# The second mixture's early results: kept in DRAM and scattered after the gathers

## The chip, the core and the metric

The kernel runs on one core of a Trainium2 chip. The metric is the device time of one execution in microseconds: 2697.74 us is the median of three runs of the kernel before (2694.27, 2697.74 and 2700.65). A core has five engines that run side by side: TensorE (PE in the profile, with PEld for its weight loads), VectorE (DVE), ScalarE (ACT), GpSimd (POOL) and SyncE (SP). SP does no arithmetic here; it issues plain DMAs. POOL issues the indirect DMAs, those with an index for each of 128 rows, and does little else. [...]

## The reference, cut to what matters

Two graph layers and two mixtures of experts alternate on 6250 nodes of 256 features (100,000 edges). The change lies in the last two of the four:

```python
x = x + _L1_gnn_ref(_layernorm(x), edge_index, W, att_src, att_dst, bias)   # attention over each node's edges
x = x + _L1_ffn_ref(_layernorm(x)[None], Wg, bg, W1, b1, W2, b2)[0]         # mixture, 8 experts, the best 2

def _L1_ffn_ref(x, Wg, bg, W1, b1, W2, b2):
    gate_logits = xf @ Wg + bg
    top_w, top_i = jax.lax.top_k(gate_logits, 2)
    top_w = softmax(top_w)
    ...
    for e in range(8):
        h = gelu(xf @ W1[e] + b1[e])                 # 256 -> 1024
        out = out + w_dense[:, e:e+1] * (h @ W2[e] + b2[e])   # 1024 -> 256
```

## The kernel before, in words

**Stages.** The first layers, their routing and the preparation of the edges come first. `gnn1` then writes a table `t1_d` to DRAM: for each node its projected features, its attention scores and its x. Nodes are sorted by degree into 49 tiles of 128, and tile t needs `CAPS[t]` gathers (8 to 41, 813 in all), one for each edge place. The stage of the change, `ffn1` (from L1202), does the attention and the second mixture in one pipelined loop. At its end the output stage (L1383 on, tiles `yg`) adds the two results that each node has in `parts` and writes `out`.

**One step of the loop** (s = 0, 1, ...; `while` at L1290) does a bit of several things, and the order is written out by hand for all engines (`manual_schedule`): each engine gets its instructions in the order in which the code makes them.
- `gather` (L1004): POOL gathers the node's own row (`own`, L1010) and then K = `CAPS[t]` tiles of 128 rows into `g` (L1020) for the tile of this step. After each gather `between()` takes one item from `outbox`. What is left in `outbox` after the last gather is issued with a small memset `gap` ahead of each (L1369).
- The attention of the tile gathered one step before (`q1`): `scores` and `shares` on DVE and ACT, `messages` on DVE (L1065), and `total` on PE (L1071, L1074), two matmuls for each gather, into `sums`.
- The end of the attention for the tile before that (`q2`): `result` on DVE, layer norm (its square root on ACT, L368), the normed `xn` (L1317), two transposes on PE (`pT`, L1320), and the gate's logits (L1225).
- Every few steps a group of four tiles is complete. `choose`, `count`, `place` and `listed` find its two experts for each node and their places (`slot`, L617), and eight row scatters `f_rows<-rw,slot` (L625), two for each tile, are put into `outbox` for the next step. They write the normed rows into a table with a region for each expert. A later group makes more blocks of 256 rows due (`moe.due`), and `written` turns their list (`blk`) on PE (L684).
- One block of 256 rows of one expert for each step, in three steps one after another. As `new`: SP fetches its rows `xr` (L697), `bcol` (L699), `ob` (L701) and the first weights w1 (1 MB, L1231), and ACT and PE turn the rows (`bxn` L1267, `bxT` L711). As `cur`: SP fetches the second weights w2 (1 MB, L1238), and `inner` (L1248, 32 matmuls `ph`) and the gelu on ACT (L1252) make `hT`. As `prev`: `outer` (L1259, 32 matmuls `py`), and `put` (L734 on ACT, L735 and L737 on DVE) makes the two results `by`. A DMA of SP also waits for the one issued eight before it.
- `sends`: the two scatters `f_parts<-by,btok` of the block (L742) are put into `outbox` for the next step. `btok` (L726) holds for each row the place in `parts`; each place is written once.

PE's order in a step is thus: `py`, two `pT`, `ph`, four `pT`, the gate, `sums`. There are 49 steps with gathers (0 to 48) and 56 blocks. A group is gathered every four steps, so its eight row scatters are in the queue of every fourth step: 16, 20, 24, ... 48. Block 0 is put at step 15 and the next ones from step 19 on, one a step. After step 48 no gathers are left; the last small groups are chosen, `nulls` (L641) fills the rest of the experts' regions, and the remaining blocks follow one a step, to step 73.

**Buffers.** `g` has 5 (two for each step from K = 14 on), `own` 4, `by` 4, w1 and w2 two each, `xr`, `bcol` and `ob` 4 each.

Of the kernel before, what the change touches and what calls it, by code (L numbers as in the profile page):

```python
# [9 lines left out]
F32 = mybir.dt.float32  # L10
BF16 = mybir.dt.bfloat16
I32 = mybir.dt.int32
# [7 lines left out]
P = 128  # L20
# [15 lines left out]
def gnn_moe_kernel(ctx: ExitStack, tc: tile.TileContext, a: dict, out: bass.AP):  # L36
    nc = tc.nc
    x, src, dst = a["x"], a["src"], a["dst"]
    N, D = x.shape
# [13 lines left out]
    dram = ctx.enter_context(tc.tile_pool(name="dram", bufs=1, space=DRAM))  # L53
# [432 lines left out]
    NTB = NB // P  # L486
# [5 lines left out]
    class Routed:  # L492
# [218 lines left out]
            nc.scalar.copy(xT, pT)  # L711
            return xT

        def places(self, pool, xr, bcol, j):

            w = pool.tile([P, NTB], F32, name="bw", bufs=4)
            first = pool.tile([P, NTB], F32, name="bfirst", bufs=4)
            nc.vector.tensor_scalar(first, xr[:, :, C_E0], bcol[:, self.n_c : self.n_c + 1], None, op0=OP.is_equal)
            nc.vector.tensor_mul(w, xr[:, :, C_WD], first)
            nc.vector.tensor_add(w, w, xr[:, :, C_W1])  # L720
            tok = pool.tile([P, NTB], I32, name="btok", bufs=6)

            off = pool.tile([P, NTB], F32, name="boff", bufs=4)
            nc.vector.tensor_scalar(off, xr[:, :, C_TOK], float(NT * P), float(j * NB), op0=OP.is_ge, op1=OP.mult)
            nc.vector.tensor_add(off, off, xr[:, :, C_TOK])
            nc.vector.scalar_tensor_tensor(tok, first, float(self.part), off, op0=OP.mult, op1=OP.add)  # L726
            return w, tok, first
# [474 lines left out]
    def ffn1(tab, bias_b):  # L1202
        NX, _, HD = a["L1_ffn_W1"].shape
        NM = HD // P
        with tc.tile_pool(name="f1", bufs=1) as fp, tc.tile_pool(name="f1r", bufs=2) as rp, \
# [9 lines left out]
            moe = Routed("f1", NX, b1c, fp, node_s, own=True)  # L1215
            with tc.tile_pool(name="f1p", bufs=2, space=PSUM) as psum:
# [11 lines left out]
                def fetch(li, j):  # L1228
                    e, xr, bcol, ob = moe.fetch(hp, li, j, a["L1_ffn_b2"])
                    w1 = wp.tile([P, 2, HD], F32, name="w1")  # L1230
                    nc.sync.dma_start(  # L1231
                        w1, a["L1_ffn_W1"][bass.ds(e, 1)].rearrange("e (k p) h -> p (e k) h", p=P))
                    return dict(li=li, j=j, xr=xr, bcol=bcol, ob=ob, w1=w1)
# [20 lines left out]
                def outer(b):  # L1254
                    pys = []
                    for i in range(NTB):
                        py = psum.tile([P, D], F32, name="py", bufs=2)
                        for m in range(NM):
                            nc.tensor.matmul(py, b["hT"][:, m, i * P : (i + 1) * P], b["w2"][:, m, :],  # L1259
                                             start=(m == 0), stop=(m == NM - 1))  # L1260
                        pys.append(py)
                    return pys

                def plain(b):
                    xn = hp.tile([P, NTB, D], F32, name="bxn")
                    for i in range(NTB):
                        nc.scalar.activation(xn[:, i, :], b["xr"][:, i, :D], AF.Identity,  # L1267
                                             bias=b["xr"][:, i, C_S : C_S + 1], scale=b["xr"][:, i, C_R : C_R + 1])
                    return xn
# [4 lines left out]
                seq = []  # L1274
# [7 lines left out]
                ready = []  # L1282
                done = 0
                new = cur = prev = None
                q1 = q2 = None
                group = None
                outbox, sends, coming = [], [], []
                gap = fp.tile([1, 1], F32, name="gap")
                s = 0
                while s < len(seq) or ready or new or cur or prev or q1 or q2 or group or outbox or coming:  # L1290

                    prev, cur = cur, new
                    new = fetch(*ready.pop(0)) if ready else None
# [5 lines left out]
                    if prev is not None:  # L1299
                        pys = outer(prev)  # L1300

                    if q2 is not None:
                        grp, i = q2["grp"], q2["i"]
# [22 lines left out]
                    if n_c:  # L1326
                        messages(q1, 0)
                    if prev is not None:
                        for r in range(NTB):
                            sends.append(partial(moe.send, *moe.put(hp, prev, r, pys[r])))  # L1330
                        prev = None
                    if new is not None:
                        xn_b = plain(new)
                    if cur is not None:
# [12 lines left out]
                    if group is not None:  # L1347
                        moe.count(small, st)
                    if new is not None:
                        new["w"], new["tok"], new["first"] = moe.places(hp, new["xr"], new["bcol"], new["j"])  # L1350
                    for c in range(1, n_c):
                        messages(q1, c)
                        total(sums, q1, c)
# [17 lines left out]
                    ready, coming = ready + coming, []  # L1371
                    outbox, sends = sends, []
                    if group is not None:
# [3 lines left out]
                        coming = [(li, j) for j in range(done, max(done, group["due"]))]  # L1377
                        done = max(done, group["due"])
                    group = q2["grp"] if q2 is not None and q2["end"] else None
                    q1, q2 = q0, q1  # L1380
                    s += 1

        with tc.tile_pool(name="f1o", bufs=3) as op_:  # L1383
            for g, n in groups:
                y = op_.tile([P, 2, n, D], F32, name="yg")
                k = min(n, NFULL - g)
                for c in range(2):
                    r = c * moe.part + g * P
# [22 lines left out]
    tab, bias_b = gnn1(moe0)  # L1411
    whole.__exit__(None, None, None)
    ffn1(tab, bias_b)


# [27 lines left out]
```

## Time and profile before

| what | value |
|---|---|
| median of three runs | 2697.74 us |
| the profiled execution, its own time | 2696.66 us |
| its span (first to last instruction) | 2694.9 us |
| granted TensorE clock, mean | 0.847 |
| DMA, mean | 171 GB/s (460.38 MB) |
| first and last gather of `ffn1` on POOL (start) | 932.5 and 2229.0 us |
| last `py` of the blocks, last result scatter | 2625.5 and 2627.3 us |
| f_parts scatters of both mixtures | 220, of which 112 in `ffn1` |
| f_rows scatters of both mixtures | 196, of which 98 in `ffn1` |

The starts of `own` on POOL (L1010) mark the steps. Those with eight row scatters began at (us):

| step | 20 | 24 | 28 | 32 | 36 | 40 | 44 | 48 |
|---|---|---|---|---|---|---|---|---|
| start | 1359.4 | 1462.1 | 1569.1 | 1680.4 | 1796.7 | 1916.9 | 2045.2 | 2184.6 |
| gathers K of the step | 15 | 16 | 17 | 18 | 18 | 20 | 21 | 25 |

How to read the profile: a group line gives line, engine, operation, out<-in and count, then busy us and mean ns of one, then the idle time of the engine ahead of it and what ended that. "issue" means that the engine waited for nothing the profile shows. A window line gives the busy time of each engine in a stretch. A timeline line gives start, duration and instruction. A time without a unit is in us from the start of the span.

### The profile page before, as it was taken

How to read it: one execution, taken by the hardware profiler on the slowest of the kernel's cores; microseconds unless marked ns; L12 is line 12 of the kernel's file. 1: busy time of each engine (PE TensorE's matmuls, PEld its weight loads, DVE VectorE, ACT ScalarE, POOL GpSimd, SP SyncE). 2: the span in 40 equal slices, each digit the busy share in tenths (PEclk: the TensorE clock that was granted, in tenths of full speed). 3: DMA queues.
4: the chain of work that ended last, by engine and by line, in shares of the span. 5: the costliest groups of instructions: out<-in, count | busy, mean ns of one | idle time of the engine just before them, and what ended most of it. 6: DMA issues, size and time to landing. Idle time of an engine off the chain costs nothing.

```text
span 2694.9 us, 30819 instructions
## 1 busy us (share of the span) xinstructions
PE 1898.8 (70%) x8479; PEld 1583.5 (59%) x8480; DVE 1214.4 (45%) x4429; ACT 904.7 (34%) x1857; POOL 1495.9 (56%) x1710
## 2 busy tenths in 40 slices
PE   4744766673974645356589889797877786899990
PEld 3522655563763433245478778676766675688880
DVE  6676554450326344255456455464444444211212
ACT  2344544441432311012234334243332323334330
POOL 4356566544760177767777777777777772111110
PEclk9855887886987876667799999898989897999995
DMA  6322555465758443444656666656565653555548
GB/s 195 96 54 59 167 166 174 147 198 149 226 168 284 135 116 107 108 126 116 213 185 218 207 205 212 195 180 202 181 213 181 187 165 124 168 193 183 203 139 287
DMA packets 334775, 460.38 MB, mean 171 GB/s; under 512 B 67566, under 2 KB 275221, under 8 KB 334599
## 3 DMA queue, kind: packets, MB, share of 16 engines
q1 hardware_dynamic: 242576, 254.25, 29.9%
q0 software_dynamic: 72304, 186.97, 23.0%
q10 hardware_dynamic: 19718, 17.15, 2.0%
q8 instruction: 69, 1.13, 0.2%
q14 instruction: 108, 0.88, 0.1%
HBM read 371.06 MB, written 87.16 MB: 170 GB/s over the span
## 4 chain that ended last, share of the span: by engine, by line
PE 23%; POOL 15%; DMA 8%; issue 8%; DVE 5%; ACT 5%; SPq 0%; DVEq 0%; POOLq 0%; ACTq 0%
POOL g L1020 11%; PE ph L1248 9%; PE py L1259 8%; PE sums L1074 5%; DMA g<-t_d,idx 4%; POOL f_rows L625 3%; DMA yg<-f_parts 2%; ACT L368 1%; DMA own<-t_d,node_i 1%; ACT L1252 1%; ACT L1044 1%; ACT bxn L1267 1%; DVE g L1065 1%; ACT hT L1252 1%; PE pT L709 1%
## 5 line engine op out<-in xcount | busy, mean ns | idle before, releaser
L1020 POOL DMA_INDIRECT g<-t_d,idx x813 | 778.7, 958 | 249.3 <-issue 230.1
L1248 PE MATMUL ph<-bxT,w 128*128 128x256 f32 x1792 | 427.3, 396 | 26.4 <-ACT hT L1252 26.3
L742 POOL DMA_INDIRECT f_parts<-by,btok x220 | 215.1, 978 | 402.2 <-DVE by L737 230.6
L1248 PEld LDWEIGHTS ph<-bxT,w 128*128 128x128 f32 x1792 | 352.0, 200 | 89.1 <-ACT hT L1252 39.4
L1259 PE MATMUL py<-w,hT 128*128 128x256 f32 x1792 | 400.9, 382 | 3.2 <-DMA w<-in_L_ffn_W 3.2
L1074 PE MATMUL sums<-g,ident 128*128 128x256 f32 x1626 | 390.5, 400 | 4.3 <-DVE g L1065 4.3
L1259 PEld LDWEIGHTS py<-w,hT 128*128 128x128 f32 x1792 | 341.6, 192 | 50.0 <-DMA w<-in_L_ffn_W 3.5
L1074 PEld LDWEIGHTS sums<-g,ident 128*128 128x128 f32 x1626 | 326.6, 203 | 62.5 <-DVE g L1065 13.4
L625 POOL DMA_INDIRECT f_rows<-rw,slot x196 | 195.4, 997 | 185.0 <-DMA ob<-in_L_ffn_expert_b 57.4
L735 DVE SCALAR_TENSOR_TENSOR by<-ob,bw,by 128x256 f32<-128x256 f32 x220 | 101.5, 481 | 409.1 <-ACT by L734 407.3
L1252 ACT ACTIVATE hT<-ph,bcol 128x256 f32<-128x256 f32 x448 | 184.6, 472 | 143.3 <-PE ph L1248 136.7
L1065 DVE TENSOR_TENSOR g<-g,weights 128x2048 f32<-128x2048 f32 (+6 forms) x88 | 229.4, 2608 | 0.0
L1320 PE MATMUL pT<-ident,xn 128*128 128x128 f32 x98 | 25.5, 352 | 288.5 <-DVE xn L1317 288.5
L1044 ACT ACT_TABLE_LOAD x36 | 46.2, 1283 | 510.5 <-DVE lg L1043 366.4
L1320 PEld LDWEIGHTS pT<-ident,xn 128*128 128x128 f32 x98 | 12.9, 170 | 303.5 <-issue 295.3
L1035 DVE TENSOR_TENSOR lg<-g,own 128x32 f32<-128x32 f32 (+6 forms) x88 | 17.1, 197 | 361.9 <-DMA g<-t_d,idx 275.7
L734 ACT ACTIVATE by<-py,bw 128x256 f32<-128x256 f32 x220 | 95.6, 474 | 199.0 <-PE py L1259 148.9
L840 PE MATMUL ph<-h,w 128*128 128x256 f32 x432 | 112.7, 419 | 64.2 <-ACT h L843 64.2
L840 PEld LDWEIGHTS ph<-h,w 128*128 128x128 f32 x432 | 90.2, 212 | 82.8 <-ACT h L843 68.7
L843 ACT ACTIVATE h<-ph,bcol 128x256 f32<-128x256 f32 x216 | 89.4, 470 | 118.1 <-PE ph L840 65.5
L406 PE MATMUL proj<-we,xT 128*128 128x264 f32 x392 | 113.4, 434 | 15.0 <-ACT xT L382 14.2
L840 PE MATMUL ph<-bxT,w 128*128 128x256 f32 x432 | 114.4, 424 | 10.4 <-ACT bxT L711 10.0
(308 smaller groups left out, 2704.4 us busy)
## 6 DMA issues: line engine op xcount, KB each, us to landing
w<-in_L_ffn_W SPq DMA_DIRECT2D x112, 1024.0 KB
w<-in_L_ffn_expert_w SPq DMA_DIRECT2D x162, 256.0 KB
xr<-f_rows SPq DMA_DIRECT2D x110, 264.0 KB
g<-t_d,idx POOLq DMA_INDIRECT x813, 2.8
yg<-f_parts ACTq DMA_DIRECT2D x12, 896.0 KB
yg<-f_parts SPq DMA_DIRECT2D x12, 896.0 KB
ob<-in_L_ffn_b SPq DMA_DIRECT2D x56, 128.0 KB
ob<-in_L_ffn_expert_b SPq DMA_DIRECT2D x54, 128.0 KB
```

The lines of the kernel that those rows point to most:

```text
L406: nc.tensor.matmul(ph, xT[:, k, :], we[:, k, :], start=(k == 0), stop=(k == 1))
L625: put = nc.gpsimd.indirect_dma_start(out=self.table[:, :], out_offset=bass.IndirectOffsetOnAxis(ap=slot[:np_, c, i : i + 1], axis=0), in_= ...
L734: nc.scalar.activation(y, py, AF.Copy, scale=w)
L735: nc.vector.scalar_tensor_tensor(y, b["ob"], w, y, op0=OP.mult, op1=OP.add)
L742: put = nc.gpsimd.indirect_dma_start(out=self.parts[:, :], out_offset=bass.IndirectOffsetOnAxis(ap=tok, axis=0), in_=y, in_offset=None,)
L840: nc.tensor.matmul(ph[:, m, :], b["ws"][i][:, k, m * P : (m + 1) * P], hi[:, k, :], start=(k == 0), stop=(k == 1))
L1020: nc.gpsimd.indirect_dma_start(out=g[:, k, :], out_offset=None, in_=halves(tab), in_offset=bass.IndirectOffsetOnAxis(ap=idx[:, o : o + 1], ...
L1065: nc.vector.tensor_mul(gv, gv, al[:, k0 : k0 + m, :, None].to_broadcast([P, m, H, C]))
L1074: nc.tensor.matmul(po, ident, g[:, k, :D], start=False, stop=k0 + k == q["K"] - 1)
L1248: nc.tensor.matmul(ph[:, q, :], b["w1"][:, k, m * P : (m + 1) * P], b["xT"][:, k, :], start=(k == 0), stop=(k == 1))
L1252: nc.scalar.activation(hT[:, m, :], ph[:, q, :], AF.Gelu, bias=b["bcol"][:, m : m + 1])
L1259: nc.tensor.matmul(py, b["hT"][:, m, i * P : (i + 1) * P], b["w2"][:, m, :], start=(m == 0), stop=(m == NM - 1))
```

## The change

A result of a block that is put before step 48 is no longer scattered in the next step. SP stores its two halves as they are into a new DRAM tensor `late_y`, and the block's number goes into a list `kept`. From step 51 on, two blocks a step are taken from that list: SP reads each back in one DMA into a new tile `late` (4 buffers), and their four scatters go into `sends`, behind the two of the current block. The row numbers have to live that long, so `places` writes them into one tile `toks` for all blocks. The loop also runs on while `kept` is not empty.

```diff
-        def places(self, pool, xr, bcol, j):
+        def places(self, pool, xr, bcol, j, tok=None):
...
-            tok = pool.tile([P, NTB], I32, name="btok", bufs=6)
+            if tok is None:
+                tok = pool.tile([P, NTB], I32, name="btok", bufs=6)
...
-                outbox, sends, coming = [], [], []
+                outbox, sends, coming, kept = [], [], [], []
+                y_d = dram.tile([moe.n_blocks * P, NTB, D], F32, name="late_y")
+                toks = fp.tile([P, moe.n_blocks, NTB], I32, name="toks")
+
+                def fetch_kept(j):
+                    y = hp.tile([P, NTB, D], F32, name="late", bufs=4)
+                    nc.sync.dma_start(y, y_d[j * P : (j + 1) * P])
+                    return [partial(moe.send, y[:, i, :], toks[:, j, i : i + 1]) for i in range(NTB)]
...
                     if prev is not None:
-                        for r in range(NTB):
-                            sends.append(partial(moe.send, *moe.put(hp, prev, r, pys[r])))
+                        ys = [moe.put(hp, prev, r, pys[r]) for r in range(NTB)]
+                        if s < len(seq) - 1:
+                            for r in range(NTB):
+                                nc.sync.dma_start(y_d[prev["j"] * P : (prev["j"] + 1) * P, r, :], ys[r][0])
+                            kept.append(prev["j"])
+                        else:
+                            sends += [partial(moe.send, *y) for y in ys]
                         prev = None
+                    if s > len(seq) + 1:
+                        for _ in range(2):
+                            if kept:
+                                sends += fetch_kept(kept.pop(0))
...
-                        new["w"], new["tok"], new["first"] = moe.places(hp, new["xr"], new["bcol"], new["j"])
+                        new["w"], new["tok"], new["first"] = moe.places(hp, new["xr"], new["bcol"], new["j"],
+                                                                        toks[:, new["j"], :])
```

More of the change, by code (lines that the diff above doesn't have):

```diff
@@ L1286, in ffn1 @@
                 group = None
-                outbox, sends, coming = [], [], []
+                outbox, sends, coming, kept = [], [], [], []
[5 more added lines that the diff above has]
+                    return [partial(moe.send, y[:, i, :], toks[:, j, i : i + 1]) for i in range(NTB)]
                 gap = fp.tile([1, 1], F32, name="gap")
                 s = 0
-                while s < len(seq) or ready or new or cur or prev or q1 or q2 or group or outbox or coming:
+                while s < len(seq) or ready or new or cur or prev or q1 or q2 or group or outbox or coming or kept:
                     prev, cur = cur, new
```

## The prediction

> **What bounds the kernel now.** First I read busy time and groups on the page. No engine is full over the span, so the shares only say that two stages must be kept apart.
>
> ```profile
> PE 1898.8 (70%) x8479; PEld 1583.5 (59%) x8480; DVE 1214.4 (45%) x4429; ACT 904.7 (34%) x1857; POOL 1495.9 (56%) x1710
> ...
> L1020 POOL DMA_INDIRECT g<-t_d,idx x813 | 778.7, 958 | 249.3 <-issue 230.1
> ```
>
> The gathers' idle time is "issue", 0.30 us before each: part of their price. A gather costs 0.95 + 0.30 = 1.255 us (in the POOL timeline 15 of them with nothing between took 18.8 us). A scatter between gathers costs about 1.3: a step of 17 gathers and 2 scatters takes 24.1 us, one of 17 and 10 takes 34.5. Second, windows cut at the start of every fourth tile, and the tail:
>
> ```profile
> 1496.00:1604.00 108.00, 96.83 (x457) 83.27 (x456) 56.08 (x187) 41.17 (x77) 82.10 (x86) 0.95 0.64 204
> ...
> 2086.00:2230.00 144.00, 109.52 (x492) 93.56 (x492) 63.77 (x187) 41.38 (x77) 109.52 (x115) 0.89 0.59 184
> ...
> 2348.00:2604.00 256.00, 256.00 (x1223) 225.44 (x1221) 50.37 (x180) 103.53 (x234) 37.75 (x72) 1.00 0.58 198
> ```
>
> Columns after the length: PE, PEld, DVE, ACT, POOL, then granted clock, DMA share, GB/s. In the first, 86 POOL instructions at 1.26 us fill the 108 us: POOL never rests. But PE is busy 97 of 108. At the last gathers (second row) PE has room. In the tail PE is full (14.25 us a block) and POOL nearly free. Third, the timelines around one step with row scatters (step 24: `own`, 16 gathers, 2 result scatters, 8 row scatters), POOL, then DVE, then PE; columns are start, duration, and in brackets the idle time before it and what ended it:
>
> ```profile
> 1462.09 0.95 POOL L1010 DMA_INDIRECT own<-t_d,node_i  x1 [0.30 <-DMA g<-t_d,idx]
> ...
> 1464.59 0.98 POOL L742 DMA_INDIRECT f_parts<-by,btok  x1 [0.30 <-issue]
> ...
> 1469.70 0.98 POOL L625 DMA_INDIRECT f_rows<-rw,slot  x1 [0.30 <-DVE start L670]
> ...
> 1496.61 0.95 POOL L1010 DMA_INDIRECT own<-t_d,node_i  x1 [0.30 <-issue]
> ```
>
> ```profile
> 1455.48 0.48 DVE L737 SCALAR_TENSOR_TENSOR by<-xr,bfirst,by 128x256 f32<-128x256 f32 x1
> ...
> 1467.29 0.17 DVE L617 CAST slot<-slot_f 128x8 int32<-128x8 f32 x1
> ```
>
> ```profile
> 1466.04 3.70 PE L1074 MATMUL sums<-g,ident 128*128 128x256 f32 x16
> ...
> 1494.41 7.07 PE L1259 MATMUL py<-w,hT 128*128 128x256 f32 x32
> 1509.34 0.66 PE L1320 MATMUL pT<-ident,xn 128*128 128x128 f32 x2 [7.86 <-DVE xn L1317]
> 1509.79 9.60 PE L1248 MATMUL ph<-bxT,w 128*128 128x256 f32 x32
> ```
>
> Two things to see. `slot`, which every row scatter needs, is ready at 1467.46, 2.3 us before PE's sums of step 23 end; the first row scatter comes at 1469.70. So POOL is only 2.2 us from waiting for PE. And after the long step PE idles 7.86 us: `ph` starts 12.6 us (12.1 to 13.2) after the step's first gather (`own`), because the layer norm's chain waits for the previous tile's landing.
>
> **What the Trainium skill says.** "DMA: Bandwidth & Descriptors", section "Issuing engines are not separate DMA queues": DMAs of all issuing engines run on the same 16 engines. So a store on SP frees POOL's time, not transfer time; the trace agrees as far as it goes (share 0.64 with both kinds running). Same page, "Anatomy of one DMA — SWDGE (gpsimd) path": about 2.0 us + bytes/436e3, 2.3 us for 128 KB; here row scatters land in 2.5 us (median), result scatters in 3.5. "TensorE: Matmul & The Clock Gate", "Part 1": after an idle window of 3.4 us PE runs at half clock. The trace agrees: 32 `ph` matmuls after the 7.86 us idle take 9.6 us, otherwise 8.3 including a wait for ACT.
>
> **The change part by part.** *Removed from POOL.* Blocks reach `put` one per step; by the loop, those put at steps 15 and 19 to 47 are kept: 30 blocks, 60 scatters, two each in the queue of steps 16 and 20 to 48. All are before the last gather (2229). At 1.3 us each: 78 us of POOL time. The new kernel's instruction order has these POOL entries gone, the other entries as they were, and 60 stores on SP.
>
> *What of it reaches the end.* A PE step costs 7.05 (`py`) + 8.3 (`ph`) + 0.6 (small ones) + 0.43K + 0.85 (sums of the tile before, K gathers): 23.7 us at K=16, where POOL alone would now need 17 x 1.255 = 21.3. POOL runs ahead, and its in-order queue then stands at the first row scatter until `slot`; every gather behind it waits. From there a loop closes over four steps, in which neither engine can gain on the other: from `slot`, the rest of POOL's long step (all but its first two gathers, 2.5 us); 12.6 from the next `own` to `ph`; 9.9 (a cold `ph`, 9.3, and small ones); that step's sums; two full PE steps; and the next `slot`, 2.3 before the sums end. POOL's own need is today's cycle (from the `own` of one long step to that of the next) less 8 x 1.3 = 10.4. The longer of the two counts:
>
> | cycle (steps) | today | POOL alone | loop | taken |
> |---|---|---|---|---|
> | 20-23 | 102.7 | 92.3 | 102.1 | 102.1 |
> | 24-27 | 107.0 | 96.6 | 104.6 | 104.6 |
> | 28-31 | 111.3 | 100.9 | 107.2 | 107.2 |
> | 32-35 | 116.3 | 105.9 | 109.7 | 109.7 |
> | 36-39 | 120.2 | 109.8 | 110.5 | 110.5 |
> | 40-43 | 128.3 | 117.9 | 114.8 | 117.9 |
> | 44-47 | 139.4 | 129.0 | 118.7 | 129.0 |
>
> (Loop at 24-27: POOL's long step 21.3 + 8 x 1.31 = 31.8, less 2.5 = 29.3; 29.3 + 12.6 + 9.9 + 7.7 + 23.7 + 23.7 - 2.3.) Today 825.2, then 781.0: 44.2. In the last two cycles K is 20 to 24, POOL's need is the longer one again, and the full 10.4 come through; in the first ones, K 15 to 17, next to nothing does. Step 48 loses its two scatters (2.6), step 16 gains 1.7 (its slot comes at about 1274.1, the row scatter at 1275.8). From that 2.7 goes at the start, where the first loop begins with POOL 3 us nearer to PE than in the steady cycle, and at the crossing between loop and POOL: **45.8 us**. So some 32 us of the 78 turn into POOL waiting for PE, mostly before step 40.
>
> *Added: 60 stores on SP.* SP issues a DMA in 0.37 us; the store waits for `by`. Behind it in SP's queue stand the next block's `xr`, `bcol`, `ob` and both weights; ACT (`bxn`) and PE (`ph`, `py`) wait for those. `by` is there at 1455.96, and the next w1 has to wait for its buffer until `ph` ends at 1461.3 anyway. Cover 5 us: cost 0, at most some us should a store come last. Bytes stay: 128 KB through SP for 128 KB through POOL. `by` is now freed by the store's landing, needed two steps later: 0. `toks` is written at another place by the same instruction: 0; the order shows no new wait.
>
> *Added: the late part.* At steps 51 to 65 SP reads 2 x 256 KB after w2, and POOL scatters four more per step: 6 x 1.3 = 7.6 us of 14.25. Traffic grows by 1.05 MB per 14.25 us, 74 GB/s on 198: share about 0.58 x 272/198 = 0.80. A w2 lands 6.7 us after its issue (last completion update in the trace) and has 13 us until `py` uses it; the reads are behind it in the queue. 15 steps at 0: the cover is 6 us a step, each us beyond it would cost 15. The late buffers (4) come free 12 us before SP wants them: their scatters are issued about 7 us after a `py` ends, land 3.5 later, and SP comes back 23 us after it. A late scatter waits for its read; behind it on POOL stand only result scatters, for which nothing waits before the output stage at 2630. At step 52 alone the last group's row scatters stand behind four late ones, but they wait for `xr` of that step anyway (2322), 20 us later. The late list is empty at step 65 of 75, so the end is not moved. Bounds for the late part: 0 to 15 us; I take 0.
>
> *Stretch 2230 to 2348* hangs on the last gather and moves along: 0.
>
> Sum: profiled execution 2696.66 (span 2694.9) - 45.8 = 2650.9. The profile lies 1.1 below the median of the runs: **2652**.
>
> **Rivals.** (a) All 78 us come through, 2620: POOL names no wait, and the model for PE might be too slow. Against it: the slack of 2.2 us and PE's 97 of 108. (b) PE's loop is slower: if the 12.6 is 14 and `ph` 9.0, each of the seven loops is 2 to 4 us longer, which leaves 22 to 36 us: 2668. For it: PE's idle times and so its clock may fall otherwise; against: less idle, a warmer clock. (c) Slower: in the tail the reads and four scatters share the engines with the weights, w2 lands after its 13 us, and PE stops in 15 blocks. It takes over from a landing of 13 + 45.8/15 = 16 us; at 17 us the time is 2652 + 15 x 4 = 2712. For it: the 10.4 us that one w2 needs today in the crowded stretch at 2321; against: a share of 0.80, and the order of the queue. (d) The change is only a shift in POOL's work: it is one, 112 result scatters in both, but to where POOL is idle; nothing beyond that.
>
> **How the numbers follow.** Forecast 0.68 (2640 to 2664); (a) or between 0.12; (b) 0.13; (c) or a loss of another kind 0.07. A measurement of this kernel tells about 0.2%, 5.4 us. (b) carried far gives "same" 0.05. Faster 0.88, slower 0.07. The range takes the main case and the near parts of (a) and (b): 2626 to 2678.
>
> **What would show it.** Right: last gather near 2184 instead of 2229; `f_rows` waiting for DVE (slot) by several us in the long steps up to 36, none at 44 and 48; PE idle before `pT` L1320 still in the step after each long one; step 44 to 48 at 129 us; the tail still 14.25 us a block with PE full and POOL 6 scatters. Wrong: (a) shows no POOL wait at `f_rows`; (b) PE steps above 24.5 at K=16; (c) `py` waiting for `w` in the tail, or SP waiting for DVE `by` while PE waits for `w`.

## The result, and the profile after

| | before | after |
|---|---|---|
| median of four runs | 2697.35 us | **2652.59 us** (2650.39 to 2661.15) |
| profiled execution, own time (span) | 2696.66 us (2694.9) | 2650.39 us (2648.7) |
| first `own` of `ffn1` | 932.5 | 931.4 |
| last gather | 2229.0 | 2181.6 |
| last `py` of the blocks | 2625.5 | 2578.7 |
| last result scatter | 2627.3 | 2580.5 |

Gathers and scatters are given by their start, the last `py` by its end. The ratio is 0.984 with a 95% interval of 0.9815 to 0.9864. The change takes 44.8 us off. The gather stage, from the first `own` to the last gather, took 1296.5 us before and 1250.2 us now: 46.3 us less. From the last gather to the last `py` it was 396.5 us and is 397.1 us. So all of the gain lies ahead of the last gather, and the late part costs nothing that can be seen.

**Busy time and groups on the page of after.** Lines from the change on stand up to 19 lower than before: L1021 is the gather, L1249 `ph`, L1260 `py`, L1329 the transposes of `xn`, L743 the result scatter.

```profile
PE 1901.9 (72%) x8479; PEld 1589.0 (60%) x8480; DVE 1215.3 (46%) x4429; ACT 904.2 (34%) x1857; POOL 1496.3 (56%) x1770
...
L1021 POOL DMA_INDIRECT g<-t_d,idx x813 | 775.8, 954 | 248.8 <-issue 228.2
...
L625 POOL DMA_INDIRECT f_rows<-rw,slot x196 | 195.3, 996 | 215.5 <-DVE ci L656 58.9
...
L743 POOL DMA_INDIRECT f_parts<-by,toks x52 | 49.9, 959 | 209.2 <-DVE by L738 155.0
```

POOL's busy time over the span is the same as before (1496 us): nothing was saved on POOL, 60 scatters were moved. The 60 instructions more are the small memsets ahead of the late scatters. The row scatters are as many as before, but POOL is idle for longer ahead of them: 215.5 us, and 185.0 us before.

**The timeline of POOL in after, around step 24** (start, duration, in brackets the idle time before and what ended it):

```profile
1453.61 1.01 POOL L1011 DMA_INDIRECT own<-t_d,node_i  x1 [0.30 <-issue]
1454.92 1.13 POOL L1021 DMA_INDIRECT g<-t_d,idx  x1 [0.30 <-issue]
1466.86 0.98 POOL L625 DMA_INDIRECT f_rows<-rw,slot  x1 [10.81 <-DVE ci L656]
1468.14 0.97 POOL L1021 DMA_INDIRECT g<-t_d,idx  x1 [0.30 <-issue]
...
1496.07 0.95 POOL L1011 DMA_INDIRECT own<-t_d,node_i  x1 [0.30 <-issue]
```

Before, the two result scatters stood between the first gather and the first row scatter, and POOL never rested. Now POOL arrives at the row scatter early and stands there for 10.8 us. POOL took its entries in the order of its queue, so the 15 gathers behind the scatter, which don't need `slot`, stood as well. What it waits for is `slot`; DVE wrote it here, in the timeline of DVE:

```profile
1466.40 0.17 DVE L617 CAST slot<-slot_f 128x8 int32<-128x8 f32 x1
```

It is ready at 1466.57, and POOL goes on 0.29 us later. The profile names `ci` (L656), which ended closest to the scatter's start; what the scatter reads is `slot`.

**The timeline of PE in after, the same step and the next:**

```profile
1469.79 7.07 PE L1260 MATMUL py<-w,hT 128*128 128x256 f32 x32
...
1493.24 7.07 PE L1260 MATMUL py<-w,hT 128*128 128x256 f32 x32
1507.99 0.66 PE L1329 MATMUL pT<-ident,xn 128*128 128x128 f32 x2 [7.68 <-DVE xn L1326]
```

From one `py` to the next, a step with the sums of 16 gathers, are 23.45 us. The gap of 7.68 us after the long step is still there (7.86 before). DVE shows where it comes from: its first operation on the tile gathered in the long step had to wait for that tile's landing, and `xn`, which DVE makes after it, was only begun at 1507.44.

```profile
1501.04 0.26 DVE L1036 TENSOR_TENSOR lg<-g,own 128x32 f32<-128x32 f32 x1 [11.36 <-DMA g<-t_d,idx]
```

So POOL waits for PE by way of `slot`, and one step later PE waits for POOL by way of a tile's landing: the loop of the prediction.

**Waits of POOL in after, 1360 to 2186** (us in total, times, longest):

```profile
POOL g L1021 <- issue: 149.3, 490, 0.3
POOL f_rows L625 <- DVE ci L656: 34.2, 6, 10.8
```

Beyond the 0.3 us of issue, the first row scatter waited 2.8 us in step 16, 5.2 in step 20, then 10.5, 8.3, 5.8 and 2.7 us in step 36: **35.3 us**, and none in steps 40, 44 and 48. (`e1` and `e7` below, with the same gather part, have 35.6 and 35.4 us.) Step 48, in POOL's timeline of after:

```profile
2139.76 0.95 POOL L1011 DMA_INDIRECT own<-t_d,node_i  x1 [0.31 <-issue]
2141.01 0.95 POOL L1021 DMA_INDIRECT g<-t_d,idx  x1 [0.30 <-issue]
2142.26 0.98 POOL L625 DMA_INDIRECT f_rows<-rw,slot  x1 [0.30 <-issue]
```

78 us removed, less 35.3 us of new waiting, is 42.7 us; measured are 44.8 us.

**Windows of after: the steps 24 to 27, the tail with late scatters, the tail without** (after the length: PE, PEld, DVE, ACT, POOL, granted clock, DMA share, GB/s):

```profile
1453.60:1560.30 106.70, 94.70 (x449) 81.32 (x447) 59.08 (x197) 43.73 (x83) 73.06 (x76) 0.97 0.67 205
2301.30:2486.50 185.20, 185.20 (x886) 163.37 (x885) 36.44 (x130) 74.70 (x170) 78.14 (x150) 1.00 0.79 264
2486.50:2571.60 85.10, 85.10 (x406) 75.09 (x405) 15.96 (x54) 33.35 (x76) 12.56 (x24) 1.00 0.53 174
```

First row: POOL has 76 instructions of 1.26 us in 106.7 us and is no longer full, and PE with 94.7 us is not full either. Each waits for the other. Second row: six scatters a block make POOL 78 of 185 us busy, the DMA share rises to 0.79, and PE is busy for all of the 185.2 us.

### The profile page after: what moved, and what is told of

Read it like the earlier page. It is cut to its first block, busy times and chain, and to the rows that moved or that the text cites. A ratio compares the mean times of both kernels' runs of the same rounds, so it can differ in the third digit from the quotient of the medians.

```text
span 2648.7 us, 31052 instructions
## 1 busy us (share of the span) xinstructions
PE 1901.9 (72%) x8479; PEld 1589.0 (60%) x8480; DVE 1215.3 (46%) x4429; ACT 904.2 (34%) x1857; POOL 1496.3 (56%) x1770
## 4 chain that ended last, share of the span: by engine, by line
PE 30%; POOL 11%; DMA 7%; issue 6%; ACT 6%; DVE 4%; ACTq 0%; SPq 0%; DVEq 0%; POOLq 0%
PE ph L1249 10%; PE py L1260 10%; POOL g L1021 10%; PE sums L1075 7%; DMA g<-t_d,idx 4%; DMA yg<-f_parts 2%; ACT L1253 1%; POOL f_rows L625 1%; ACT bxn L1268 1%; ACT L368 1%; ACT hT L1253 1%; PE pT L709 1%; ACT L1045 1%; PE sums L1072 1%; PE pT L1329 0%
## 5 line engine op out<-in xcount | busy, mean ns | idle before, releaser
L1021 POOL DMA_INDIRECT g<-t_d,idx x813 | 775.8, 954 | 248.8 <-issue 228.2
L1249 PE MATMUL ph<-bxT,w 128*128 128x256 f32 x1792 | 429.0, 398 | 25.9 <-ACT hT L1253 25.8
L1249 PEld LDWEIGHTS ph<-bxT,w 128*128 128x128 f32 x1792 | 354.3, 201 | 88.1 <-ACT hT L1253 38.6
L1260 PE MATMUL py<-w,hT 128*128 128x256 f32 x1792 | 400.8, 383 | 3.8 <-DMA w<-in_L_ffn_W 3.8
L1260 PEld LDWEIGHTS py<-w,hT 128*128 128x128 f32 x1792 | 342.1, 192 | 49.9 <-DMA w<-in_L_ffn_W 4.0
L625 POOL DMA_INDIRECT f_rows<-rw,slot x196 | 195.3, 996 | 215.5 <-DVE ci L656 58.9
L1329 PE MATMUL pT<-ident,xn 128*128 128x128 f32 x98 | 25.8, 356 | 242.7 <-DVE xn L1326 242.7
L743 POOL DMA_INDIRECT f_parts<-by,toks x52 | 49.9, 959 | 209.2 <-DVE by L738 155.0
L1329 PEld LDWEIGHTS pT<-ident,xn 128*128 128x128 f32 x98 | 13.5, 172 | 256.1 <-issue 248.1
L743 POOL DMA_INDIRECT f_parts<-by,btok x108 | 106.6, 987 | 90.6 <-DVE by L736 62.5
L844 ACT ACTIVATE h<-ph,bcol 128x256 f32<-128x256 f32 x216 | 89.1, 470 | 114.8 <-PE ph L841 62.7
```

Source lines behind the costliest of these rows:

```text
L625: put = nc.gpsimd.indirect_dma_start(out=self.table[:, :], out_offset=bass.IndirectOffsetOnAxis(ap=slot[:np_, c, i : i + 1], axis=0), in_= ...
L743: put = nc.gpsimd.indirect_dma_start(out=self.parts[:, :], out_offset=bass.IndirectOffsetOnAxis(ap=tok, axis=0), in_=y, in_offset=None,)
L844: nc.scalar.activation(ho[:, m, :], ph[:, m, :], AF.Relu, bias=b["bcol"][:, 2 * i + m : 2 * i + m + 1])
L1021: nc.gpsimd.indirect_dma_start(out=g[:, k, :], out_offset=None, in_=halves(tab), in_offset=bass.IndirectOffsetOnAxis(ap=idx[:, o : o + 1], ...
L1249: nc.tensor.matmul(ph[:, q, :], b["w1"][:, k, m * P : (m + 1) * P], b["xT"][:, k, :], start=(k == 0), stop=(k == 1))
```

## The experiments

Theory A is the prediction's: 78 us of POOL time are removed; where POOL then stands at the first row scatter until PE's chain has given `slot`, a cycle is as long as the loop through both engines, and the gain is lost there; stores and late reads cost nothing. Rivals: the rest of the 78 us was eaten by the stores and reads (B), or the saving is worth the same part everywhere, 57% of each scatter (C). The kernels of one group shared a chip: the first four with a before of 2695.07 us, the last four with one of 2694.95 us. All edits but that of `e3` are made to the kernel after.

**e1_no_store_no_read** leaves out the 60 stores and the 30 late reads. Its late scatters send a tile of zeros, so the kept results are not in the output.

```diff
+                fill = fp.tile([P, NTB, D], F32, name="fill")
+                nc.vector.memset(fill, 0.0)
...
-                    y = hp.tile([P, NTB, D], F32, name="late", bufs=4)
-                    nc.sync.dma_start(y, y_d[j * P : (j + 1) * P])
+                    y = fill
...
-                            for r in range(NTB):
-                                nc.sync.dma_start(y_d[prev["j"] * P : (prev["j"] + 1) * P, r, :], ys[r][0])
```

> The change without its 60 stores and 30 reads: the late scatters send a constant tile instead (the kept blocks' results are left out). Theory (stores and reads lie beside other work, POOL and PE set the pace): 2649 to 2656 us, as the changed kernel's 2652.6; last gather at 2180 to 2187 us, tail 14.25 us a block. Rival (stores hold up SP's fetches, or the reads the weights): 2652.6 less what they cost, 2640 or below.

Measured: 2650.67 us, ratio 0.9836 (0.9821 to 0.9851), against 0.984 for the change. The waits at the row scatters are the same, 35.6 us, and so is the gather stage, 1250.2 us in both. B falls: it needed some 33 us. The medians put stores and reads together at 0 to 2 us, and the two intervals leave room for some 9 us. Of the late reads the tail says more, from the last gather to the last `py`: 395.9 us without them, 397.1 with them, 396.5 before. Among the other kernels with two late blocks a step at most it lies between 396.1 and 398.5, so 1 or 2 us can't be told.

**e2_rows_last** holds the row scatters back. In the queue of the long step they come after its last eight gathers instead of its first eight; no-op places are put ahead of them. Everything else is the kernel after.

```diff
-                        outbox += moe.scatters(group["n"], group["rw"], slot, group["pad"])
+                        rows = moe.scatters(group["n"], group["rw"], slot, group["pad"])
+                        k_next = CAPS[seq[s + 1][0]["g"] + seq[s + 1][1]] if s + 1 < len(seq) else 0
+                        outbox += [lambda: None] * max(0, k_next - len(outbox) - len(rows)) + rows
```

> The change, and the eight row scatters of a long step are taken up at its last eight gathers and not at its first eight, so that POOL reaches the first of them some 10 us later. Theory (about 32 of the 78 us saved on POOL are spent waiting for slot at the first row scatter): the wait goes and the rest of the 78 us comes through: last gather near 2151 us, 2616 to 2626 us, no POOL wait at f_rows in the long steps. Rival (PE's own pace is the limit, not the place where POOL waits for it): 2645 to 2653 us, POOL waiting elsewhere, for g buffers.

Measured: **2607.93 us** (2603.17 to 2612.5), ratio 0.9678 (0.9665 to 0.9691). That is faster than the kernel after, clear of its interval, and faster than I expected. The first row scatter of the same group, in POOL's timeline of this kernel:

```profile
1446.80 0.95 POOL L1021 DMA_INDIRECT g<-t_d,idx  x1 [0.30 <-PE sums L1075]
1448.05 0.98 POOL L625 DMA_INDIRECT f_rows<-rw,slot  x1 [0.30 <-DVE start L665]
```

It does not wait any more. What ended POOL's idle time before the row scatters of the whole stage, first after (us, times), then this kernel:

```profile
  DVE ci L656: 39.0, 8
  issue: 23.5, 77
  DVE sel L668: 12.1, 1
```

```profile
  issue: 24.1, 79
  DVE ci L656: 4.7, 1
```

The waits of after sum to 48.5 us beyond the issue time, those of `e2` to 4.4: 44.1 us less. The gather stage went from 1250.2 to 1205.6 us: 44.6 us. So the lost part of the gain was this wait. It does not move elsewhere, either: ahead of the gathers POOL waits 1.4 us beyond the issue time in the whole stage (1.0 in after), and PE's wait for `xn` fell from 72.0 to 40.5 us in the same stretch. What is left is POOL's own pace. From `own` to `own`, the seven cycles from step 20 on take 92.0, 96.3, 101.5, 106.1, 109.5, 117.9 and 128.6 us here: the prediction's column "POOL alone" to within 0.6 us. The size that I missed is that of steps 7 and 11: they too have eight row scatters in the queue, and wait 1.4 and 11.8 us beyond issue in after, ahead of the first kept block. Only 4.4 us of that is left here. I had counted only the steps from 16 on.

**e3_before_rows_last** is the same edit made to the kernel before, where every result is still scattered at once.

> The same late place for the row scatters in the kernel before the change. Theory: POOL waits nowhere there, so nothing is gained: 2693 to 2702 us. Rival (late row scatters help by themselves, by looser coupling): 2685 us or below.

Measured: 2684.28 us, ratio 0.9955 (0.994 to 0.997). I had expected next to nothing, so this is a miss, and the number is that of the rival. POOL's timeline of the kernel before, and then of this one, shows where the 10.8 us come from:

```profile
1152.41 0.95 POOL L1020 DMA_INDIRECT g<-t_d,idx  x1 [0.30 <-PE pT L1320]
1165.72 0.99 POOL L625 DMA_INDIRECT f_rows<-rw,slot  x1 [12.36 <-DVE sel L668]
```

```profile
1156.95 0.95 POOL L1020 DMA_INDIRECT g<-t_d,idx  x1 [0.30 <-issue]
1162.67 0.98 POOL L625 DMA_INDIRECT f_rows<-rw,slot  x1 [4.77 <-DVE ci L656]
```

The kernel before already had the same stall in step 11, where no block has been put yet and the queue holds no result scatters: 12.1 us beyond issue, and 2.3 us in step 7. Of these 14.4 us 4.5 are left, and the gather stage is 11.5 us shorter (1285.0 us). From step 16 on, where result scatters filled POOL's time, there was no wait to take away: from `own` to `own`, the cycles from step 20 on are as before to within 0.5 us. So late row scatters help by themselves, as the rival has it, but only where POOL stood waiting for `slot`. And `e2` against `e3`, the change with the wait nearly gone on both sides, is 76.4 us by the medians and 79.4 by the gather stages: within the noise all of the 78 us that it takes off POOL.

**e4_keep_from_35** and **e5_keep_to_31** each apply the change to some of the blocks only: those put at steps 35 to 47 (26 scatters), or those up to step 31 (28 scatters).

```diff
-                        if s < len(seq) - 1:
+                        if 35 <= s < len(seq) - 1:
```

> Only the blocks put at steps 35 to 47 are kept (13 blocks, 26 scatters out of the queue of steps 36 to 48). Theory by the table of loops: 10.4 us for each of the cycles from 40 and 44, 8 to 10 for that from 36, 2.6 for step 48: 32 to 34 us, 2662 to 2668 us. Rival (every scatter taken out is worth the same, 45/60 us): 26 of them 19.5 us, 2678 us.

Measured: 2663.14 us, ratio 0.9879 (0.9864 to 0.9894), 31.9 us less than before. 26 x 1.3 = 33.8 us were removed: nearly all of it comes through. In `e5` the condition is `s < 32`.

> The mirror of keeping from step 35: only blocks put up to step 31 are kept (14 blocks, 28 scatters out of the queue of steps 16 to 32). Theory: at K of 14 to 17 the loop between PE and POOL takes back nearly all: 7 to 9 us, 2686 to 2691 us, with POOL waiting some 29 us for slot at the row scatters of steps 16 to 32. Rival (all scatters are worth the same): 28 of 60, 21 us, 2676 us.

Measured: 2691.81 us, ratio 0.9986 (0.9974 to 0.9998). About as many scatters are removed as in `e4`, and 3 us come of it (the interval has 0.5 to 7), a little less than the 7 to 9 of A, whose range it misses by 0.8 us. What ended POOL's idle time before the row scatters from 1250 on in `e5`:

```profile
  DVE ci L656: 33.6, 5
```

28 x 1.3 = 36.4 us removed, less 32.1 us of waits beyond the issue time: 4.3 us. The gather stage of the profiled execution is 6.8 us shorter than before (1289.7 us). C would have given both some 20 us and falls twice. The two gains and the six scatters of neither (7.8 us) sum to 42.8 us, near the 44.8 of the change.

**e6_half_py** asks whether it is PE that holds up `slot`. It leaves out half of the second layer's matmuls, 16 of 32 `py` a block, up to step 48; those blocks' results lack half of their sum.

```diff
-                def outer(b):
+                def outer(b, n_m=NM):
...
-                        for m in range(NM):
+                        for m in range(n_m):
...
-                                             start=(m == 0), stop=(m == NM - 1))
+                                             start=(m == 0), stop=(m == n_m - 1))
...
-                        pys = outer(prev)
+                        pys = outer(prev, NM // 2 if s < len(seq) else NM)
```

> The change, with half of the second layer's matmuls left out while gathers run (16 py matmuls a block for 32, up to step 48; half of the hidden width is left out there): a PE step is 3.5 us shorter. Theory (POOL's wait is for PE's pace): POOL waits less for slot, some 15 us in place of 34, the last gather comes about 18 us earlier, near 2163 us, and the time is 2632 to 2637 us. Rival (POOL is held by something that PE's matmuls don't set): 2652 us.

Measured: 2636.88 us, ratio 0.9785 (0.9768 to 0.9801). What ended POOL's idle time before the row scatters, from 1250 to 2160:

```profile
  DVE ci L656: 20.8, 7
```

18.7 us are left of 35.3, 16.6 less, and the gather stage is 15.5 us shorter than in after (1234.7 us). POOL's instructions are the same; a shorter PE step shortens POOL's wait and the time by about the same amount.

**e7_four_late** tests the tail's reserve: four kept blocks a step instead of two.

```diff
-                        for _ in range(2):
+                        for _ in range(4):
```

> The change with four kept blocks a step in the tail in place of two: ten scatters a step, 12.7 us of POOL in 14.25, 1.05 MB more a step, 346 GB/s asked for in place of 272. The gather part is as in the changed kernel. Theory of the cover: two blocks a step cost nothing because the engines of DMA have room; four ask for more than the 290 GB/s that any slice of the profile reached, so w2 comes late in the 7 to 8 steps that have late work: 3 to 20 us more, 2655 to 2673 us. Rival (the transfers have more room than the slices show): 2652 us, PE without a gap in the tail.

Measured: 2664.48 us, ratio 0.9891 (0.987 to 0.9912). The tail from the last gather to the last `py` grew from 397.1 to 406.4 us. PE stopped four times for weights, 7.1 us in all; two of the stops, in PE's timeline:

```profile
2334.65 7.17 PE L1260 MATMUL py<-w,hT 128*128 128x256 f32 x32 [1.28 <-DMA w<-in_L_ffn_W]
...
2351.67 7.17 PE L1260 MATMUL py<-w,hT 128*128 128x256 f32 x32 [2.50 <-DMA w<-in_L_ffn_W]
```

SP's queue (`SPq`) stood at the late reads (L1294, from 2250 on), whose four buffers their scatters had not yet freed:

```profile
SPq L1294 <- DMA f_parts<-late,toks: 53.0, 23, 5.9
```

The next block's loads stand behind those reads: w1 was issued 1.8 to 6.6 us after `ph` had freed its buffer, at first at intervals of 15.3 to 17.3 us where a block takes 14.25. A w2 landed 9.7 to 12.5 us after its issue while late blocks were read, where it took 7.4 to 9.1 in after. From 2301 to 2410 the DMA share was 0.86, and 0.97 in its fullest 15 us. So at four blocks a step the tail is over the edge, and not quite in the way of rival (c): no landing took the 13 us that a w2 has in after. At the four stops w2 was issued only 8.0 to 10.3 us ahead of where `py` could have started, and took 9.9 to 12.5 us. By these figures it took both, the late issue and the crowded transfers: with 13 us to land none of the four would have been late, and none with a landing of 7.8 us (the last of them only just). A kernel with more `late` buffers would test that, and was not run.

**e8_rows_after_4** is `e2` with only four gathers more ahead of the row scatters, `min(4, ...)` in the number of no-op places.

> Row scatters taken up four gathers (5 us) later in each long step, between the changed kernel (none, 2652.6) and that with them at the last eight gathers (2607.9). Theory: POOL still waits where it waited more than 5 us, that is about 7 us in all in steps 20 to 32 and 2 to 3 us in step 11: 9 to 10 us above the latest place, 2614 to 2621 us. Rival (the gain goes with the number of gathers delayed, of 4 to 9 possible): half way, about 2630 us.

Measured: 2626.02 us, ratio 0.9744 (0.9725 to 0.9764), which lies between the two expectations. The waits before the row scatters of the whole stage are these, of 0.3 us issue each:

```profile
  DVE ci L656: 19.9, 5
```

That is 18.4 us beyond issue, 14.0 more than in `e2`. The gather stage is 1220.8 us, 15.2 longer. So wait and time move together here too; I had put the waits at half their size. The time alone doesn't exclude the rival (2630 us); the waits account for it without the rival.

The gather stage over the runs, with the waits at row scatters beyond issue: after 1250.2 us with 48.5, `e8` 1220.8 with 18.4, `e2` 1205.6 with 4.4. From each to the next, the two differences agree within 1.3 us.

## Why the prediction was right, point by point

The forecast was 2652 us (2640 to 2664), and 2652.59 was measured. The terms below are right to a few us; that the sum is right to less than one is luck in part, since the four runs alone spread over 10.8 us.

- **78 us off POOL.** Right. With the wait gone on both sides it is worth 76.4 us (`e2` against `e3`). 1.3 us a scatter holds.
- **Some 32 us turn into waiting for `slot`, mostly before step 40.** Right: 35.3 us, in steps 16 to 36, none from 40 on. That the wait takes the gain is shown by `e2` (take the wait away), `e4` and `e5` (where a scatter is removed decides its worth), and `e6` (a faster PE gives part of it back).
- **The length of the loop.** Right to 1% in each cycle. It runs from one `slot` to the next, so it is read from first row scatter to first row scatter: 103.0, 104.2, 106.7, 108.9 and 109.9 us in the first five cycles, for 102.1, 104.6, 107.2, 109.7 and 110.5 predicted. From `own` to `own`, as the table had them, they are 97.4, 106.7, 109.2, 112.0 and 112.6 us. Its parts fit as well, in the cycle from step 24: 29.2 us from the first row scatter to the next `own` (29.3 predicted), 12.4 from there to `ph` (12.6), and 62.7 from there to the next first row scatter (62.7). The fifth cycle is not the loop's, though: no wait stands at step 40, and 109.9 us is POOL's own need (109.8), which lay only 0.7 us under the loop. The table mixed two marks: POOL's wait comes after `own`, so from `own` to `own` a cycle holds the wait at its beginning (5.2 us in the first) and not the one at its end (10.5). Over the five the difference shrinks to the first wait less the last: 538.0 us measured, 534.1 predicted.
- **The cycles that POOL sets.** Right: 117.0 and 128.6 us for 117.9 and 129.0.
- **The 2.7 us taken off at the start and the crossing.** Right in sum. From the start of step 20 to that of step 48 were 825.3 us before and are 783.6 us now, 41.7 less, for 44.2 - 2.7 = 41.5 predicted. Step 48 itself, to the last gather, is 2.6 us shorter, as predicted.
- **1.7 us gained at step 16.** Not shown. From the first `own` to step 20 the stage is 2.1 us shorter than before (424.8 for 426.9), but it is as short in `e4` (424.5), which keeps no block so early. Terms of this size can't be settled from single profiles.
- **60 stores on SP at 0.** Right as far as `e1` can tell. SP's waits in after from 1360 to 2250, while stores are made, show the cover:

```profile
SPq L1341 <- DVE by L738: 542.6, 49, 24.3
SPq L1232 <- PE ph L1249: 69.1, 21, 28.7
```

  L1341 is the store: SP stands at it for `by`, and in 21 cases it still has to stand at a w1 (L1232) until `ph` frees the buffer. There the store held up no weights. Of the other steps this line says nothing; there `e1` decides.
- **The late part at 0.** Right. A block still takes 14.25 us, PE never rests in the window of the tail, the share is 0.79 (0.80 predicted), and a w2 lands 7.8 us after its issue (median in that window; 6.9 before), with 13 us to do so. The Trainium skill's statement ("DMA: Bandwidth & Descriptors", "Issuing engines are not separate DMA queues") that all issuers share the 16 engines is what this rests on, and the share agrees: it rose by about the bytes added, from 0.58 to 0.79, though SP issued the reads and POOL the scatters. The 2.3 us that the prediction has from the same page is an estimate by the page's fit for a POOL DMA of 128 KB; the trace before had 2.5 and 3.5 us, and the sum used the 3.5. `e7` shows that the reserve ends between two and four kept blocks a step.
- **Rivals.** (a), all 78 us, would have been right if POOL had had no wait to fall into, and `e2` is that kernel. (b), a slower loop, is excluded by the cycles. (Its 22 us were too few: by the table, loops 4 us longer lengthen the first five cycles and the sixth by 0.9, which leaves 25.) (c) does not show in after; in `e7` PE stops for weights, but the late issue has its part in that. (d) is what the change does: POOL's work is moved, not less (1496 us in both).
- **What it overlooked.** It said that "POOL names no wait". In the two long steps ahead of the change's stretch the kernel before did wait, 14.4 us, at the same row scatter. That changed no number of the prediction, since the change leaves those steps as they are; it made two of the expectations too small.

The Trainium skill's "TensorE: Matmul & The Clock Gate", "Part 1", has idle windows of PE cost it clock, and the traces agree in direction. The mean grant over steps 24 to 27 is 0.95 before and 0.97 after, where PE's longest gap there is 7.86 and 7.68 us, and 1.00 in `e2`, where it is 0.93 us. No run separates what this is worth.

## What to carry to other kernels

Before work is removed from an engine that "never rests", ask what it will wait for next; here a removed scatter was worth nearly its whole time in steps 36 to 48 and almost nothing up to step 32. Find the first entry in its in-order queue that depends on another engine, measure how early that dependence is met today (2.2 us here), and follow the loop from there. If the entry can be moved back behind work that depends on nothing, do that together with the saving: here the moving was worth 10.8 us alone, the saving 44.8 alone, and both 87.1. Moving work to a stretch where its engine is idle adds to what the engine that is full there depends on: ask whether its loads come to stand behind the moved work in a queue, and whether the DMA engines have room for both. Two blocks a step were free here; four made the tail 9 us longer.

## What the runs showed of the hardware

In the tail the DMA engines carried 264 GB/s at a share of 0.79 for 185 us, with PE fed 2 MB of weights every 14.25 us and not once short; a 1 MB load took 7.8 us (median), only 0.9 us longer than at a share of 0.58. I had kept a risk for that. Over 109 us of `e7`, at 287 GB/s and 0.86, the same load took 9.7 to 12.5 us beside the late blocks, and PE stopped. A row scatter that waited 10.8 us for `slot` kept 15 gathers waiting that didn't need it. The profile named the wait at a row scatter after `ci` or `sel`, instructions of DVE that the scatter doesn't read and that end close to the one that it does read (`slot`, 0.29 us earlier in step 24).
